# Output projections by seven half-sized block products, with the tick rebuilt for pairs of batches

## The chip, the cores and the metric

The kernel runs on one core of one Trainium2 chip. The time is device microseconds of one execution; medians of several executions are given, all in the fast state (runs within 1.5% of the fastest one of the same kernel). The kernel keeps all arithmetic in f32. Five engines matter: TensorE (PE; PEld is its weight load), VectorE (DVE), ScalarE (ACT), GpSimd (POOL) and the queue that starts transfers (SP).

## The reference, cut to what matters

128 graphs of 128 nodes with 512 features. Layer 0 is a transformer layer whose scores are multiplied by the adjacency matrix; layer 1 is a graph attention layer. Both are residual, with layer norm and a Relu ahead.

```python
# layer 0
h = relu(layernorm(x)); q, k, v = h @ Wq.T + bq, h @ Wk.T + bk, h @ Wv.T + bv   # 512 x 512 each
attn = softmax(q k^T * scale * (adj + adj)) per head (8 heads of 64)
x = x + (attn v) @ Wo.T + bo
# layer 1
h = relu(layernorm(x)); Wh = h @ W                                              # 512 x 512
e = leaky_relu(Wh a1 + (Wh a2)^T); e = where(adj > 0.5, e, -9e15)
x = x + elu(softmax(e, axis=1) @ Wh)
```

Both kernels reassociate layer 1: they first gather (attention times h) and then project with W. So each batch has five 512 x 512 projections: q, k, v, the output projection with Wo, and the last one with W.

## The kernel before

q, k and v are already done in the cheaper way: for a group of four batches, each of the three products is split into 2 x 2 blocks and formed from seven block products instead of eight (Winograd's form of Strassen's scheme). Sums of blocks are made on VectorE beforehand, and the results are put together from three banks of PSUM (the tiles `acc_a`, `acc_b` and `acc_c`, into which the products are accumulated). The 21 products ("units" q0 to v6) are strewn over the ticks of the group before, so that TensorE always has something independent to do. The output projections are plain:

```python
    def rows_matmul(lhsT, w):
        pm = ps1.tile([P, E], F32, name="pm", tag="ps1")
        for c in range(C):                       # 4 products of 128 x 512, f32
            nc.tensor.matmul(pm, lhsT[:, c, :], w[:, c, :], start=(c == 0), stop=(c == C - 1))
        return pm
    ...
        def done():                              # what follows a unit of q, k, v
            if n == 0:
                first(0, 0)                      # ScalarE: copy with bias out of bank "a"
            elif n == 1:
                add(0, 0, "b")                   # VectorE: add bank "b"
            ...
            elif n == 4:
                first(1, 1)                      # ScalarE, and then
                add(1, 1, "c")                   # VectorE, which waits for it
```

The schedule is written by hand, one tick per batch; in the trace VectorE runs its instructions in the order of the source (L380, L381 and L259, shown below, start at 1009.90, 1010.17 and 1010.43 us). The beginning of a tick (t is in attention, t-2 in layer 1):

```python
            if 0 <= t - 2 < B:
                scores1(t - 2)
                softmax1(t - 2)
            if t < B:
                scores(t)
                mask(t)
            done = unit(0)
            ...
            if 0 <= t - 2 < B:
                scale1(t - 2)        # scaling of the layer 1 attention w, needed by gather1
            done()                   # the end of unit 0, after it
            if t < B:
                exps(t)
            ...
            unit(1)()
            ...
            unit(2)()
            if 0 <= t - 2 < B:
                gather1(t - 2)       # TensorE: h2 times w
```

## Time and profile before

| | before |
|---|---|
| median | 2659.05 us (2658.74 to 2661.01, 3 runs) |
| TensorE busy, whole span / 100 to 2500 us | 98% / 100% |
| VectorE, ScalarE busy | 69%, 43% |
| period of four batches in the steady part | 81.14 us |
| clock of TensorE | 0.997 |

In this trace the granted clock of TensorE is 0.50 in a few stretches only: 3.41 us from 64.8 us on, 3.41 from 2607.8, 6.81 from 2641.9 and the last 0.25; from 68.3 to 2607.7 us it is 1.00. Such a fall to 0.50 is what the texts below mean by the clock gate, and by tripping it.

The prediction below shows the lines that carry this. This is VectorE around the scaling of w in a steady tick of the kernel before (columns: start, duration, engine, line, operation, output<-inputs, shape):

```profile
1009.90 0.15 DVE L380 RECIPROCAL rs<-sums 128x1 f32<-128x1 f32 x1
1010.17 0.34 DVE L381 TENSOR_SCALAR w<-w,rs,mv 128x128 f32<-128x128 f32 x1
1010.43 0.68 DVE L259 TENSOR_TENSOR kT<-acc_c,kT 128x512 f32<-128x512 f32 x1
```

The scaling (L381) stands ahead of the unit's add (L259), as in the source, and is done at 1010.5 us. The gather that needs it starts at 1015.95 us: over 5 us of slack. The order protected from little there: the units that begin a tick are q0, k0, k3 and k6, and of these only k6 ends with an add, which waits for no copy of its own unit.

### The profile page before, as it was taken

The numbers are of one execution on the slowest core, as the hardware profiler recorded it, in microseconds if no ns is written. First come the engines' busy times: TensorE is split into PE (matmuls) and PEld (weight loads), VectorE is DVE, ScalarE is ACT, GpSimd is POOL, SyncE is SP. The second block draws the span as 40 slices with busy tenths as digits, with TensorE's granted clock in tenths as the row PEclk, the third lists the DMA queues.
The fourth block names the chain that finished last, engine by engine and source line by source line (L and its number), as shares of the span: only waits on it lengthen the run. The fifth ranks groups of instructions, "written<-read, shape, count | busy, mean of one in ns | idle before, by whom it ended". The sixth has DMA issues, their size and how long they took to land.

```text
span 2655.8 us, 38303 instructions
## 1 busy us (share of the span) xinstructions
PE 2615.8 (98%) x13744; PEld 1882.8 (71%) x13744; DVE 1830.3 (69%) x3509; ACT 1151.3 (43%) x3595; POOL 334.7 (13%) x647
## 2 busy tenths in 40 slices
PE   7999999999999999999999999999999999999996
PEld 6677777777777777777777777777777777777763
DVE  5776767766676767677666767676776667676655
ACT  2444444444444444444444444444444444444443
POOL 1111111111111111111111111111111111111001
PEclk9999999999999999999999999999999999999999
DMA  4433322222321232222222223322222232122010
GB/s 153 68 74 70 64 64 64 65 64 66 77 56 57 74 70 64 64 65 63 64 67 77 58 54 75 69 64 64 66 62 64 67 77 58 55 75 57 31 40 20
DMA packets 209133, 173.29 MB, mean 65 GB/s; under 512 B 48432, under 2 KB 158000, under 8 KB 208560
## 3 DMA queue, kind: packets, MB, share of 16 engines
q1 hardware_dynamic: 207360, 170.84, 26.2%
q8 instruction: 109, 1.79, 0.4%
q14 instruction: 80, 0.66, 0.1%
q10 hardware_dynamic: 1584, 0.01, 0.0%
HBM read 137.11 MB, written 33.68 MB: 64 GB/s over the span
## 4 chain that ended last, share of the span: by engine, by line
PE 97%; DVE 2%; ACT 1%; DMA 1%; issue 0%; SPq 0%; ACTq 0%; DVEq 0%
PE pm L157 33%; PE acc_a L238 25%; PE acc_c L238 13%; PE acc_b L238 6%; PE sc L290 5%; PE pc L331 5%; PE pa L320 4%; PE pg L389 4%; PE pb L363 1%; ACT at L307 1%; DMA hT<-in_xT 0%; DVE at L314 0%; DVE nmx L300 0%; DVE at L296 0%; PE pt L177 0%; DMA x<-in_x 0%
## 5 line engine op out<-in xcount | busy, mean ns | idle before, releaser
L157 PE MATMUL pm<-w,gT 128*128 128x512 f32 x1024 | 464.0, 596 | 1.5 <-ACT gT L391 1.5
L157 PE MATMUL pm<-wo,cxT 128*128 128x512 f32 x1024 | 460.9, 593 | 0.5 <-ACT cxT L336 0.5
L307 ACT ACTIVATE at<-at,nmx 128x128 f32<-128x128 f32 x1024 | 395.6, 388 | 130.5 <-DVE nmx L300 130.5
L150 POOL TENSOR_SCALAR mv<-mv 128x1 f32<-128x1 f32 x256 | 117.1, 458 | 2149.8 <-DVE mv L147 2149.6
L157 PEld LDWEIGHTS pm<-w,gT 128*128 128x128 f32 x1024 | 195.4, 191 | 194.1 <-issue 185.9
L157 PEld LDWEIGHTS pm<-wo,cxT 128*128 128x128 f32 x1024 | 194.1, 190 | 191.1 <-issue 183.7
L399 DVE SCALAR_TENSOR_TENSOR x<-pm,x 128x512 f32<-128x512 f32 x128 | 88.5, 692 | 341.5 <-ACT ez L398 341.5
L398 ACT ACTIVATE ez<-pm 128x512 f32<-128x512 f32 x128 | 76.5, 598 | 399.2 <-PE pm L157 399.2
L238 PE MATMUL acc_a<-hT,wq 128*128 128x256 f32 x1024 | 246.7, 384 | 0.0
L238 PE MATMUL acc_a<-hT,wk 128*128 128x256 f32 x1024 | 245.3, 382 | 0.0
L238 PE MATMUL acc_a<-wv,hT 128*128 128x256 f32 x1024 | 244.2, 381 | 0.7 <-ACT v L250 0.7
L238 PEld LDWEIGHTS acc_a<-hT,wq 128*128 128x128 f32 x1024 | 190.7, 191 | 40.5 <-issue 14.8
L238 PEld LDWEIGHTS acc_a<-wv,hT 128*128 128x128 f32 x1024 | 189.4, 190 | 38.6 <-issue 14.8
L238 PEld LDWEIGHTS acc_a<-hT,wk 128*128 128x128 f32 x1024 | 187.2, 190 | 38.6 <-issue 14.8
L322 ACT COPY aT<-pa 128x1024 f32<-128x1024 f32 x128 | 129.6, 1012 | 147.4 <-PE pa L320 144.7
L307 ACT ACTIVATION_READ_ACCUMULATOR at<-at,nmx 128x1 f32 x1024 | 191.8, 187 | 0.0
L255 ACT ACTIVATE qT<-acc_a,bq 128x256 f32<-128x256 f32 x256 | 107.2, 470 | 194.6 <-PE acc_a L238 194.6
L145 DVE BATCH_NORM_STATS2 st<-x 128x6 f32<-128x512 f32 x256 | 176.4, 689 | 9.1 <-DMA x<-in_x 4.5
L151 POOL TENSOR_TENSOR mv<-mv,mhalf 128x1 f32<-128x1 f32 x256 | 177.3, 693 | 21.3
L331 PEld LDWEIGHTS pc<-aT,v 128*64 128x64 f32 x2048 | 109.2, 136 | 83.4 <-issue 83.4
L255 ACT ACTIVATE kT<-acc_a,bk 128x256 f32<-128x256 f32 x256 | 107.4, 471 | 134.0 <-PE acc_a L238 134.0
L314 DVE TENSOR_TENSOR at<-at,rs 128x1024 f32<-128x1024 f32 x128 | 156.8, 1225 | 4.4
(92 smaller groups left out, 3926.3 us busy)
## 6 DMA issues: line engine op xcount, KB each, us to landing
x<-in_x SPq DMA_DIRECT2D x256, 256.0 KB, 3.5
out<-x SPq DMA_DIRECT2D x128, 256.0 KB, 2.1
hT<-in_xT SPq DMA_DIRECT2D x120, 256.0 KB, 10.6
mr<-rows SPq DMA_DIRECT2D x120, 128.0 KB, 3.4
adj<-in_adj SPq DMA_DIRECT2D x128, 64.0 KB, 2.1
adjT<-in_adjT SPq DMA_DIRECT2D x128, 64.0 KB, 2.0
rows<-mv SPq DMA_DIRECT2D x120, 1.0 KB, 8.5
wq<-in_wqT SPq DMA_DIRECT2D x1, 1024.0 KB, 7.2
```

The costliest lines, as they stand in the source:

```text
L145: nc.vector.bn_stats(st, src)
L150: nc.gpsimd.tensor_scalar_add(rstd, rstd, EPS)
L151: nc.gpsimd.tensor_tensor(rstd, rstd, mhalf, OP.pow)
L157: nc.tensor.matmul(pm, lhsT[:, c, :], w[:, c, :], start=(c == 0), stop=(c == C - 1))
L238: nc.tensor.matmul(acc[:, m, :], lhsT, rhs, start=fresh and m == 0 and c == 0, stop=c == 1, skip_group_check=True)
L255: nc.scalar.activation(dst(t, f)[:, m, :], a[:, m, :], AF.Identity, bias=bias[:, j : j + 1])
L290: nc.tensor.matmul(sc[:, s * C + i, :], qT[r, i, cols], kT[r, i, cols], start=True, stop=True)
L307: nc.scalar.activation(at[:, j, :], at[:, j, :], AF.Exp, bias=nmx[:, j : j + 1], accum_out=sums[:, j : j + 1])
L314: nc.vector.tensor_tensor(at, at, rs[:, :, None].to_broadcast([P, H, S]), OP.mult)
L320: nc.tensor.transpose(pa[:, j, :], at[:, j, :], ident)
L322: nc.scalar.copy(aT, pa)
L331: nc.tensor.matmul(pc[s * D : (s + 1) * D, i, :], vs[b // G][:, b % G, head * D : (head + 1) * D], ats[b][:, s * C + i, :], start=True, st ...
```

## The change

Its intent: the two output projections, too, by seven block products. A block product needs two row blocks, so two batches go through a tick together. Now a pair's output projection is seven products of 128 x 256 over two K-blocks, instead of two times four of 128 x 512. In exchange VectorE makes the sums of blocks (`context_sums`, `gather_sums`) and adds the products up. Cut to its core:

```diff
-    def rows_matmul(lhsT, w):
-        ...
+    def product_rows(left, w, which, n):
+        la, wb, bank = PRODUCTS[n]
+        slot = 1 if bank == "b" else 0
+        own = "c" if bank == "c" else "a"
+        if n == 0 or n == 3:
+            accs[which, own] = ps1.tile([P, 2, E // 2], F32, name="row_" + own, tag="ps1")
+        acc = accs[which, own][:, slot, :]
+        for c in range(2):
+            nc.tensor.matmul(
+                acc, left[:, la, c, :], w[:, wb, c, :], start=n in (0, 3) and c == 0, stop=c == 1, skip_group_check=True
+            )
+        return acc
 ...
+    def context_sums(half):
+        token_sums(cxT, cxT[:, 4:7], (half,))
+    def output0(p, n):                                  # the adds of the first output projection
+        ...
+            if n == 0 or n == 1:
+                add(0, 0, acc)
 ...
-        nc.vector.tensor_scalar(h2, xs[b], mv[:, 0:1], 0.0, op0=OP.subtract, op1=OP.max)
+            nc.scalar.activation(h2[:, i, :], xs[p][:, i, :], AF.Relu, bias=nmr[:, i : i + 1], scale=mv[:, 1, i : i + 1])
 ...
+SEQ = "v0 v1 v2 v3 v4 q0 v5 q1 v6 q2 q3 q4 k0 q5 k1 q6 k2 k3 k4 k5 k6".split()
+            units = (SEQ[10:] if odd else SEQ[:10]) ...  # ten units in an even pair-tick, eleven in an odd one
+            if attn:
+                scores(a)                               # the mask and the maximum belong to it now
+            unit()()
+            if e is not None:
+                scores1(e)
+            if attn:
+                exps(a, range(4))
+            if o is not None:
+                first, second = output0(o, 0), output0(o, 1)
+                first()
+                second()
+            if e is not None:
+                softmax1(e)
+            if attn:
+                exps(a, range(4, H))
+            ...
+            unit()()
+            if e is not None:
+                scale1(e)
+            if o is not None:
+                output0(o, 2)()
+            done = unit()
+            if attn:
+                normalise(a)
+            done()
+            if f is not None:
+                finish_a(f)                             # final passes, one tick later than before
+            if e is not None:
+                gather1(e, 0)
+                gather1(e, 1)
+            done = unit()
+            if f is not None:
+                finish_b(f)
+            done()
 ...  (second half of the tick: batch b, products 3 to 6 of both projections, statistics, dots)
```

## The prediction

> **What bounds the kernel now.** I read the page first (busy shares, slices, chain), then the busy time of the steady stretch, the groups by form, and last the timeline of TensorE and of all engines.

> ```profile
> PE 2615.8 (98%) x13744; PEld 1882.8 (71%) x13744; DVE 1830.3 (69%) x3509; ACT 1151.3 (43%) x3595; POOL 334.7 (13%) x647
> ...
> PE 97%; DVE 2%; ACT 1%; DMA 1%; issue 0%; SPq 0%; ACTq 0%; DVEq 0%
> ```
> ```profile
> 100.00:2500.00 2400.00, 2400.00 (x12660) 1730.99 (x12659) 1683.48 (x3224) 1060.12 (x3323) 304.99 (x586) 1.00 0.27 65
> ```
> From 100 to 2500 us TensorE is busy in all 2400.00 us, at clock 1.00: it never waits, so the steady time is the sum of its passes. VectorE is busy in 70% of that stretch and ScalarE in 44%.
> ```profile
> 1007.24 1.99 PE L238 MATMUL acc_c<-hT,wk 128*128 128x256 f32 x8
> 1009.07 3.60 PE L157 MATMUL pm<-wo,cxT 128*128 128x512 f32 x8
> 1012.50 1.89 PE L238 MATMUL acc_a<-wv,hT 128*128 128x256 f32 x8
> 1014.23 1.89 PE L238 MATMUL acc_c<-wv,hT 128*128 128x256 f32 x8
> 1015.95 1.05 PE L389 MATMUL pg<-w,h 128*128 128x128 f32 x8
> 1016.84 1.89 PE L238 MATMUL acc_a<-wv,hT 128*128 128x256 f32 x8
> ```
> Read start to start: eight passes of 512 columns take 3.43 us (429 ns each), eight of 256 take 1.73 (216 ns each). A product in f32 is two passes.
> ```profile
> L307 ACT ACTIVATE at<-at,nmx 128x128 f32<-128x128 f32 x1024 | 395.6, 388 | 130.5 <-DVE nmx L300 130.5
> L314 DVE TENSOR_TENSOR at<-at,rs 128x1024 f32<-128x1024 f32 x128 | 156.8, 1225 | 4.4
> L255 ACT ACTIVATE qT<-acc_a,bq 128x256 f32<-128x256 f32 x256 | 107.2, 470 | 194.6 <-PE acc_a L238 194.6
> L366 DVE TENSOR_TENSOR w<-w,neg 128x128 f32<-128x128 f32 x128 | 36.6, 286 | 30.8 <-ACT w L365 30.8
> L259 DVE TENSOR_TENSOR v<-acc_c,v 128x512 f32<-128x512 f32 x64 | 44.0, 688 | 26.9 <-ACT v L250 23.8 <-PE acc_c L238 3.1
> ```
> These price the new small operations: on VectorE 128 columns cost 286 ns, 512 cost 688, 1024 cost 1225. So 256 columns, which do not occur before, should cost about 0.42 us (0.39 start to start).

> [...] the ratio 1:2 holds and halving a side loses nothing. [...] (1225-286)/896 = 1.05 ns per column. [...] VectorE's order in every tick is that of the source. This carries my main argument. [...] Seen here near the end: after 3.02 us of idling the next eight passes took 5.28 instead of 3.43 us, though after two equal gaps nothing happened.

> **The change, part by part.** I count in groups of four batches (two pairs), because 21 products of q, k, v belong to a group.

> *TensorE.* A batch has scores 1.09 + 0.19 of turnaround, context 1.03, the row transpose 0.25, gather 0.89, attention transpose 0.87: 4.32 us. The two output projections by the plain way are 2 x 3.43 = 6.86. A group: 4 x (4.32 + 6.86) + 21 x 1.73 = 81.05. Measured from the start of scores at 135.26 to that at 2569.39, 30 groups: 81.14. The method fits.
> After: each output projection of a pair is seven products of two K-blocks, two passes each, 28 passes of 256 columns = 6.06 us in place of 6.86. A group: 4 x 4.32 - 0.25 + 4 x 6.06 + 36.33 = 77.6. Gain 3.5 us a group, some 110 us of the run.

> *VectorE, per pair.* Added: sums of context blocks and of gathered blocks, 8 x 0.42; seven adds of output products in place of two of 684 ns, +1.57; three adds for the second projection, +1.26; the small product behind the statistics, +0.15. Gone: hidden1 moves to ScalarE (-0.96), the mask and its add become one operation (-0.6), and pairing saves on the residual, norm, shift, softmax and finishing operations (-1.3). Together +3.5 us on 28.6: 32 of some 39 us. The new small product after GpSimd's power also makes VectorE wait about 1 us a pair. ScalarE gains two Relu of 512 and four copies of 256, about +2.7 on 18. Neither becomes the bound by its sum.

> *DMA.* Bytes stay; fewer, larger transfers at a 27% share. Hidden.

> *Ends.* Before, outside those 30 groups: 2655.8 - 30 x 81.14 = 221.6. After: the weights' sums now stand ahead of the first hidden_T in VectorE's queue and wait for the load (+5); in the first two pairs some 10 us more of the output work is missing and moves to the end, and less idling is left there (-15); the drain is three pair-ticks of serial steps instead of two batch-ticks (+10). About 221. So the time is 221 + 30 x (77.6 + s), s being TensorE's new waiting in a group: 2549 with none.

> **What s is.** I followed the queues through a pair-tick in source order, with durations from the rows above. Zero is the start of the first batch's scores.

> End of an even tick: from the end E of the second attention transpose, ScalarE copies (1.0 + 0.1), makes the first half of h2 (0.7); VectorE does dots 1.36, add 0.39, dots 1.36, context_sums 0.78: E + 5.7. TensorE has two products of 0.87 and the context left: E + 2.8. So VectorE enters an odd tick 2.9 us behind TensorE. An odd tick has one more product (k6), which lets VectorE in at 1.9 in even ticks.

> Then the gather needs scale1. In an odd tick VectorE starts the mask at 2.9; mask and maximum 2.5, the new score operation 0.4; ScalarE: two Prelu 0.7, four exponentials at 0.387 = 1.55, two of the second softmax 0.8, four more 1.55, and then the two bias copies of product q4, 0.9. VectorE's add of q4 stands ahead of scale1 in its queue and must wait for those copies: 0.66, then reciprocal and scaling 0.66. TensorE starts the gather 0.26 later: at 2.9 + 10.0 = 12.9. In its own order it gets there after scores 1.1, q3 1.9, row transposes 0.35, two products 1.73, q4 1.73, one product 0.87, k0 1.73: at 9.4. It waits 3.5 us, once in each odd tick.
> In an even tick the second unit is v1, whose add waits for no late copy: scale1 is ready at about 1.9 + 7.0 = 8.9 against 9.4. No wait.
> At other places (attention transposes, sums ahead of the third output product, banks) I find slack of 0.5 to 8 us. So s = 3.5, and the gain of 3.5 a group is eaten almost whole: 221 + 30 x 81.1 = 2654.

> **The rivals.** (A) No new wait: TensorE stays gap-free, 2549. For it: all engines have room by their sums, and the order looks tuned by hand. Against it: even if VectorE began the mask as early as scores allow (1.2 instead of 2.9), the chain would end at 11.2, a wait of 1.8: 2603. (B) The waits are longer than I think: a gap of 3.5 us is in reach of the clock gate; if half the gaps cost another 1.85, +28 us: 2680. (C) VectorE becomes the bound in odd ticks (its list there: 36 us with the hidden sums and the wait for GpSimd, of 39.7): another 1.5 us a group of missed transposes or late bank releases, 2700. (D) The chain is real, but the next waits move, so that half is won back: 2600.

> **Range and chances.** The bare sum gives 2654. The clock gate pulls up, and the possibility that I misplace one wait in ScalarE's queue (an order this worked out has presumably been seen running well) pulls down harder. I say 2645, with 2590 to 2695. Faster by over 2% is below 2606: it needs s under 1.9, so 0.25. Slower by over 2% is above 2712: s above 5.4, 0.10. Within: 0.65.

> **What would show it.** Passes of 256 columns at 216 ns in both output projections: the gain exists. TensorE's steady stretch no longer fully busy, with the idle time ahead of the gather (pg), put down to VectorE's scaling of w, about 3.5 us, in every second pair-tick and not in the others: my step is right. If the gather never waits, or waits in both kinds of tick, the chain is wrong. VectorE should show 78 to 82% busy, with a wait for GpSimd of 1 us a pair; the mean clock below 0.99 would mean the gate took part. A time near 2550 overturns the argument; one above 2700 says that VectorE's queue binds at more places than this one.

## The result

| | before | after |
|---|---|---|
| median (4 runs each) | 2658.89 us | 2704.13 us |
| span of the profiled run | 2655.8 us | 2701.3 us |
| TensorE busy | 2615.8 us, 98% | 2554.2 us, 95% |
| VectorE, ScalarE busy | 69%, 43% | 76%, 48% |
| period of four batches | 81.14 us | 82.66 and 81.17 us in turn |

The ratio is 1.0173 (1.0155 to 1.0191): slower by 1.7%. Here and below a ratio is the mean time of one kernel's fast runs over that of the other's fast runs of the same rounds, so not quite the ratio of the medians. TensorE is busy for 62 us less, though some of its passes now run at half speed (below). All of that, and 45 us more, went into waiting. The slowdown is clear of noise, but smaller than the 2% at which the record calls a kernel slower.

The page of the kernel after, busy shares and chain:

```profile
PE 2554.2 (95%) x15288; PEld 2184.8 (81%) x15288; DVE 2052.4 (76%) x3781; ACT 1306.0 (48%) x3915; POOL 119.1 (4%) x263
...
PE 77%; DVE 10%; ACT 9%; issue 3%; DMA 1%; POOL 0%; SPq 0%; POOLq 0%; DVEq 0%; ACTq 0%
```

The chain that ended last (followed back from the last instruction, each step to what released it) was 97% TensorE before. Now it runs through VectorE and ScalarE for 19% of the span. This alone doesn't size the loss: in e10 below, where TensorE's steady part shows no wait, it is still 16%. Of the groups (busy time and mean ns of one, then the idle time ahead and its releaser), the new products and the gather:

```profile
L297 PE MATMUL row_a<-wo,cxT 128*128 128x256 f32 x1280 | 323.3, 383 | 10.9 <-DVE x L370 10.7
L297 PE MATMUL row_a<-w,gT 128*128 128x256 f32 x1280 | 319.2, 380 | 1.8 <-ACT z L474 0.9
L447 PE MATMUL pg<-w,h 128*128 128x128 f32 x1024 | 156.0, 316 | 97.7 <-DVE w L439 94.7
```

The block products are as fast as those of q, k and v and almost never wait. The gather (L447) waits 94.7 us in 32 places for VectorE's scaling of w (L439), and its mean pass has gone from 276 ns before to 316. Two gathers of odd pair-ticks, one after the other, with the unit that follows each:

```profile
1005.30 2.02 PE L447 MATMUL pg<-w,h 128*128 128x128 f32 x16 [2.98 <-DVE w L439]
1007.15 1.89 PE L245 MATMUL acc_a<-hA,wq 128*128 128x256 f32 x8
...
1086.47 3.50 PE L447 MATMUL pg<-w,h 128*128 128x128 f32 x16 [2.99 <-DVE w L439]
1089.82 1.89 PE L245 MATMUL acc_a<-hA,wq 128*128 128x256 f32 x8
```

Both waited the same 2.98 to 2.99 us. The first took 1.85 us to the next unit, the second 3.35: it ran at half speed. The busy times in the stretch of each of these two gathers (columns: stretch, length, busy us of PE, PEld, DVE, ACT, POOL, then clock, share of the transfer engines, GB/s):

```profile
1005.30:1008.70 3.40, 3.40 (x24) 3.22 (x25) 3.33 (x5) 1.17 (x2) 0.00 (x0) 1.00 0.00 0
1086.40:1089.80 3.40, 3.33 (x16) 3.36 (x17) 3.33 (x5) 0.58 (x1) 0.00 (x0) 0.53 0.00 0
```

The clock there is 1.00 and 0.53. In the steady part every second gap is followed by such a stretch; that is why the periods alternate between 81.17 and 82.66 us.

```profile
1000.84:1004.25 3.41, 1.47 (x7) 0.95 (x5) 0.32 (x1) 3.41 (x17) 0.00 (x0) 1.00 0.00 0
1082.76:1086.17 3.41, 0.72 (x4) 0.29 (x2) 1.03 (x3) 3.03 (x13) 0.00 (x0) 1.00 0.00 0
```

So it is in all 30 gaps from 186 to 2561 us: the 15 that tripped the clock have 2.50 to 2.70 us in one step, the 15 others 1.95 at most. This is read from one trace; no run shifted the gaps to test it. Nor is it a sharp limit: in the drain a step with two waits, 1.83 us of idling in all (2656.31 to 2659.72), tripped the clock too.

In even pair-ticks there is no wait at all:

```profile
1045.03 1.95 PE L447 MATMUL pg<-w,h 128*128 128x128 f32 x16
```

The wait itself, step by step, in one odd pair-tick that starts with the scores at 1074.04 us (engines mixed, in order of time):

```profile
1076.98 1.22 DVE L314 SCALAR_TENSOR_TENSOR at<-sc,adj 128x1024 f32<-128x1024 f32 x1
1078.23 1.22 DVE L318 TENSOR_REDUCE nmx<-at 128x8 f32<-128x1024 f32 x1
1079.37 0.41 DVE L421 SCALAR_TENSOR_TENSOR w<-adjT,pb 128x256 f32<-128x256 f32 x1
1079.81 0.69 ACT L423 ACTIVATE w<-w,ws 128x128 f32<-128x128 f32 x2 [2.40 <-DVE w L421]
...
1082.34 0.39 ACT L432 ACTIVATE w<-w,nmx 128x128 f32<-128x128 f32 x1
...
1084.26 0.81 ACT L262 ACTIVATE qT<-acc_a,bq 128x256 f32<-128x256 f32 x2
1085.11 0.69 DVE L266 TENSOR_TENSOR qT<-acc_c,qT 128x512 f32<-128x512 f32 x1 [4.15 <-ACT qT L262]
1085.71 0.15 DVE L438 RECIPROCAL rs<-sums 128x2 f32<-128x2 f32 x1
1085.90 0.42 DVE L439 TENSOR_TENSOR w<-w,rs 128x256 f32<-128x256 f32 x1
```

The second exponential of layer 1's softmax (L432) ends at 1082.7 us. From then on the scaling could run. But VectorE stands in front of q4's add (L266) for 4.15 us until ScalarE, behind four more exponentials, has made q4's copies (L262). Only then come the reciprocal and the scaling.

### The profile page after: what moved, and what is told of

It reads as the page before. It is cut to its first block, busy times and chain, and to the rows that moved or that the text cites. A ratio compares the mean times of both kernels' runs of the same rounds, so it can differ in the third digit from the quotient of the medians.

```text
span 2701.3 us, 40548 instructions
## 1 busy us (share of the span) xinstructions
PE 2554.2 (95%) x15288; PEld 2184.8 (81%) x15288; DVE 2052.4 (76%) x3781; ACT 1306.0 (48%) x3915; POOL 119.1 (4%) x263
## 4 chain that ended last, share of the span: by engine, by line
PE 77%; DVE 10%; ACT 9%; issue 3%; DMA 1%; POOL 0%; SPq 0%; POOLq 0%; DVEq 0%; ACTq 0%
PE acc_a L245 20%; PE row_a L297 16%; PE acc_c L245 10%; PE row_c L297 8%; PE acc_b L245 6%; PE pg L447 6%; PE pa L336 4%; ACT at L324 4%; PE sc L312 4%; DVE junk L409 4%; PE pc L356 4%; DVE at L314 2%; ACT aT L338 1%; ACT w L432 1%; ACT w L423 1%
## 5 line engine op out<-in xcount | busy, mean ns | idle before, releaser
L297 PE MATMUL row_a<-wo,cxT 128*128 128x256 f32 x1280 | 323.3, 383 | 10.9 <-DVE x L370 10.7
L297 PE MATMUL row_a<-w,gT 128*128 128x256 f32 x1280 | 319.2, 380 | 1.8 <-ACT z L474 0.9
L297 PEld LDWEIGHTS row_a<-wo,cxT 128*128 128x128 f32 x1280 | 236.0, 191 | 48.6 <-DVE x L370 20.6
L297 PEld LDWEIGHTS row_a<-w,gT 128*128 128x128 f32 x1280 | 236.2, 191 | 31.1 <-ACT z L474 1.7
L447 PE MATMUL pg<-w,h 128*128 128x128 f32 x1024 | 156.0, 316 | 97.7 <-DVE w L439 94.7
L262 ACT ACTIVATE kT<-acc_a,bk 128x256 f32<-128x256 f32 x256 | 106.9, 469 | 290.9 <-PE acc_a L245 290.9
L447 PEld LDWEIGHTS pg<-w,h 128*128 128x128 f32 x1024 | 149.8, 230 | 112.3 <-ACT kT L262 100.8
L262 ACT ACTIVATE qT<-acc_a,bq 128x256 f32<-128x256 f32 x256 | 106.6, 466 | 125.3 <-PE acc_a L245 125.3
L330 DVE TENSOR_TENSOR at<-at,rs 128x1024 f32<-128x1024 f32 x128 | 156.8, 1225 | 4.4
L318 DVE TENSOR_REDUCE nmx<-at 128x8 f32<-128x1024 f32 x128 | 156.2, 1220 | 4.4
L370 DVE TENSOR_TENSOR x<-row_a,x 128x256 f32<-128x256 f32 x320 | 135.2, 422 | 31.0 <-PE row_a L297 24.5
L314 DVE SCALAR_TENSOR_TENSOR at<-sc,adj 128x1024 f32<-128x1024 f32 x128 | 154.4, 1206 | 4.5 <-PE sc L312 4.5
L312 PE MATMUL sc<-kT,qT 64*128 64x128 f32 x2048 | 149.7, 286 | 0.0
L266 DVE TENSOR_TENSOR qT<-acc_c,qT 128x512 f32<-128x512 f32 x64 | 44.0, 688 | 134.0 <-ACT qT L262 130.8
```

The costliest lines, as they stand in the source:

```text
L262: nc.scalar.activation(dst(t, f)[:, m, :], a[:, m, :], AF.Identity, bias=bias[:, j : j + 1])
L297: nc.tensor.matmul(acc, left[:, la, c, :], w[:, wb, c, :], start=n in (0, 3) and c == 0, stop=c == 1, skip_group_check=True)
L312: nc.tensor.matmul(sc[:, s * C + j, :], qT[r, j, cols], kT[r, j, cols], start=True, stop=True)
L314: nc.vector.scalar_tensor_tensor(at, sc, QSCALE, adjs[p][:, i : i + 1, :].to_broadcast([P, H, S]), op0=OP.mult, op1=OP.mult)
L318: nc.vector.tensor_reduce(nmx, at, AX.X, OP.max, negate=True)
L330: nc.vector.tensor_tensor(at, at, rs[:, :, None].to_broadcast([P, H, S]), OP.mult)
```

## The experiments

Two theories stood against each other. **Queue**: one wrong place in VectorE's order costs a gap, and the gap trips the clock gate (a stretch of 3.41 us at clock 0.50 in the trace above). **Sum**: with 3.5 us more a pair VectorE is near its bound, so that a wait taken away at one place comes back at another. All ten kernels gave the right result. The median of the kernel before was 2658.9 to 2663.5 us in the four sets of rounds, so a difference of medians from different sets can be off by some 5 us; ratios and, for small differences, the periods in the traces don't have this fault.

### e1: the scaling ahead of the unit's add

```diff
-            unit()()
-
+            done = unit()
             if e is not None:
                 scale1(e)
+            done()
```

> Only the order within the second unit is changed: the scaling of w (scale1) is issued ahead of the copies and the add that end that unit. Queue theory (the gather of an odd pair-tick waits 3.1 us because scale1 stands behind the add of q4, which waits for ScalarE's copies, and every second such gap also trips the clock gate for 1.5 us): the scaling ends 2.8 us earlier, a wait of about 0.4 us is left, no gate; 2704 - 31 x 2.7 - 22 = about 2600 us. Rival, VectorE is the bound by its sum and the wait only moves: over 2670 us, with new idle time of TensorE elsewhere in the tick.

Measured: 2609.29 us, ratio to before 0.9796 (0.9779 to 0.9812). One line moved makes the kernel 95 us faster than the change as given. The odd pair-tick now:

```profile
1128.29 2.02 PE L447 MATMUL pg<-w,h 128*128 128x128 f32 x16
1130.14 1.89 PE L245 MATMUL acc_a<-hA,wq 128*128 128x256 f32 x8
1132.22 1.09 PE L336 MATMUL pa<-ident,at 128*128 128x128 f32 x8 [0.18 <-DVE at L330]
```

The gather no longer waits for anything the profile names; 0.18 us is left ahead of the attention transpose. The period is 78.72 us in every group: the alternation has gone with the gap. The queue theory's 2600 is missed by 9 us (e8 takes another 0.4 us off each group), the sum theory's "over 2670" by 60.

### e2, e3: the gather moved behind the fourth unit, alone and with e1

```diff
-            if e is not None:
-                gather1(e, 0)
-                gather1(e, 1)
             done = unit()
             if f is not None:
                 finish_b(f)
             done()
+            if e is not None:
+                gather1(e, 0)
+                gather1(e, 1)
```

> Only the gather is moved behind the fourth unit on TensorE (1.73 us of independent passes); VectorE's and ScalarE's order up to scale1 stays. Queue theory: the wait falls from 3.1 to 1.4 us in odd ticks, the gate no longer trips; 2704 - 31 x 1.73 - 22 = about 2628 us. Rival, VectorE is the bound: VectorE's order ahead of the gather is the same and it would be no faster, over 2685 us.

> Both edits together. Queue theory: no wait ahead of the gather in any tick, groups of four batches at 77.6 us; 2704 - 31 x 3.1 - 22 = about 2585 us. Rival, VectorE is the bound or the next wait stands close behind: over 2650 us, with the idle time ahead of another operation.

Measured: 2641.88 us (ratio 0.9917) and 2641.77 us (ratio 0.9916). e2 was 14 us slower than expected. e3 was 57 us slower than the queue theory had it, and worse than e1 alone: by its number alone it speaks more for the sum theory ("over 2650"). The profile of e3 shows what it is, in every odd pair-tick:

```profile
1143.49 1.99 PE L245 MATMUL acc_a<-hA,wq 128*128 128x256 f32 x8 [1.64 <-ACT qT L262]
1145.32 1.95 PE L447 MATMUL pg<-w,h 128*128 128x128 f32 x16
```

This is q5, which now comes before the gather. It accumulates on in the bank that q4's copies (L262) are still reading, and waits 1.64 us for them. e2 shows the same wait, 42.7 us in 26 places between 300 and 2400 us, as e3 does. With the gather ahead of it, this second wait had stood hidden. So it is a new wait on the same late copies, not a full VectorE, but that had to be tested: e10.

### e10: e3, with q4's copies ahead of the second four exponentials

```diff
+            done = unit(early=True)        # product 4 makes its copies at once, its add stays in done()
             if attn:
                 exps(a, range(4, H))
             if p == 1:
                 spread_u()
-            done = unit()
```

> On the kernel of e3: the two bias copies of q4 are issued on ScalarE ahead of the second four exponentials instead of behind them; nothing else moves. In e3 product q5 waits 1.64 us in each odd tick for those copies to leave its bank. If that is what e2 and e3 missed: the wait goes and no other takes its place, groups at 78.3 us, 2642 - 31 x 1.6 = about 2592 us. If the wait for the bank has another cause or a third wait stands behind it: over 2625.

Measured: 2595.36 us, ratio 0.9742 (0.9729 to 0.9755), period 78.32 us, against 79.85 in e3. The second wait was the copies' place in ScalarE's queue, and no third stood behind it.

### e4: the gap filled, not shortened

Six products of constant weights, issued into the gather's own bank, which the gather overwrites:

```diff
+        if fill:                            # odd ticks only
+            for _ in range(6):
+                nc.tensor.matmul(
+                    pg[:, 0:2, :].rearrange("p c s -> p (c s)"), wo_sb[:, 0, 0, 0:P], wo_sb[:, 1, 0, :], start=True, stop=True
+                )
```

> Nothing is moved; in odd ticks six products of constant weights (12 passes of 256 columns, 2.6 us) are issued ahead of the gather into its own bank, which the gather then overwrites. They fill the gap of 3.1 us without shortening it. Gate theory (the idle time trips the clock, which costs 1.5 us in every second group): the slow stretches in the steady part vanish, all groups at 81.2 us, 2704 - 15 x 1.5 = about 2682 us. Rival, the slow stretches have another cause (they come every 163.8 us anyway): 2704 us or more, with the half-speed gathers still there.

Measured: 2681.69 us. The edited kernel's line numbers are shifted (L448 is the filling, L452 the gather):

```profile
996.21 2.75 PE L448 MATMUL pg<-wo 128*128 128x256 f32 x12
999.36 2.02 PE L452 MATMUL pg<-w,h 128*128 128x128 f32 x16 [0.40 <-DVE w L439]
1001.22 1.89 PE L245 MATMUL acc_a<-hA,wq 128*128 128x256 f32 x8
```

The steady groups from the second on all take 81.17 us: the gap costs as much as before, but no half-speed stretch follows it. So idling causes the stretches, and in the steady part they cost 2704.13 - 2681.69 = 22 us (and 15 x 1.49 by the periods). It is a strange cure, useless work that makes a kernel faster, and a good test.

### e5, e6: the same VectorE operation added at two places

On e1's kernel, the maximum over the scores is taken twice, for the second batch of the pair (e5) or for the first (e6). It adds 1.22 us a pair-tick, 78 us of VectorE's work, either way.

```diff
-        nc.vector.tensor_reduce(nmx, at, AX.X, OP.max, negate=True)
+        for _ in range(2 if i == 1 else 1):          # e6: i == 0
+            nc.vector.tensor_reduce(nmx, at, AX.X, OP.max, negate=True)
```

> On the kernel of e1: the maximum over the scores of the second batch of every pair is computed twice (one more VectorE operation of 1.22 us a pair-tick, 78 us over the run, same result), where attention transposes have some 3 us of slack. Queue theory: at most 10 us more than e1's 2609. Rival, VectorE is the bound by its sum once the gather's wait is gone: 2609 + 64 x 1.22 = some 2685 us.

> The same operation of 1.22 us, as often, but on the first batch of the pair, ahead of the chain to the gather. Queue theory: even ticks have 0.5 us of slack and odd ones none, so 0.7 + 1.3 us a group: 2609 + 31 x 2.0 = about 2670 us, the wait ahead of the gather again. If only VectorE's sum counted, the time would equal e5's.

Measured: 2613.80 us and 2667.02 us: 5 and 58 us more than e1. The period is 78.72 us in e5, as in e1, and 80.54 in e6. VectorE is busy in 81% and 80% of the span. So its sum isn't the bound; where an operation stands decides. A part of my expectation for e6 was wrong: the wait is not ahead of the gather but earlier, at the third product of the first output projection (L371 is VectorE's add of the two products before it, out of the same bank):

```profile
505.32 1.13 PE L297 MATMUL row_a<-wo,cxT 128*128 128x256 f32 x4 [1.08 <-DVE x L371]
512.24 1.10 PE L337 MATMUL pa<-ident,at 128*128 128x128 f32 x8 [0.18 <-DVE at L331]
```

I had traced that bank in the change and found it just free in time; with 1.22 us more ahead of the adds it isn't. That the time still came within 3 us of my 2670 was luck.

### e7, e8, e9: the first pair-tick, and the best version

The ends of the run had also come out longer than predicted. In the first pair-tick of e1 VectorE stands 7.2 us (5.7 in the change as given) in front of a load (`hidden`) while the second batch's softmax waits behind it. e7 is e1 with that call moved behind the residual shift, in the first pair-tick only.

```diff
-            if h is not None:
+            if h is not None and p > 0:
                 hidden(h)
 ...
                 shift(p)
             done()
+            if p == 0:
+                hidden(h)
```

> On the kernel of e1: in the first pair-tick alone, the first use of a loaded xT (it waits 7.2 us for its transfer, in front of the second batch's softmax in VectorE's queue) is issued after the residual shift. If this wait makes the first ticks longer than I had them: the 5.6 us idle ahead of the second attention transpose goes and the half-speed stretch after it with it, 8 to 10 us: about 2600. If the first ticks are long for another reason: within 2 us of e1's 2609.

Measured: 2607.62 us, 2 us under e1: no gain worth naming. The wait had moved to the next operation in VectorE's queue that needs a transfer, the statistics of a later pair:

```profile
78.12 0.69 DVE L159 BATCH_NORM_STATS2 st<-x 128x6 f32<-128x512 f32 x1 [8.68 <-DMA x<-in_x]
```

e8 adds two edits to e7: the first batch's `normalise` also goes ahead of the second unit's add (which in e1 still waits 1.63 us for ScalarE), and the sums of w1's blocks move to the second pair-tick.

```diff
             if attn:
                 normalise(a)
+            done2()                        # the end of the second unit, now behind scale1 and normalise
             done()
 ...
-                weight_sums(w1_sb)         # at the end of the first pair-tick
 ...
+            if p == 1:
+                weight_sums(w1_sb)         # in the middle of the second
```

> The best version I can see: e1, with the normalisation of the first batch also issued ahead of the add of the second unit, e7's edit, and the sums of w1's blocks one tick later. Queue theory: groups at 78.2 us instead of 78.7 (-16), first ticks shorter (-10): about 2585 us, faster than the kernel before by 2.8%. If VectorE's queue binds elsewhere: 2600 or more.

Measured: 2594.77 us, ratio 0.9747 (0.9733 to 0.9762). The period falls to 78.32 us (78.2 expected); the first ticks gain 2 us of the 10 I had hoped for. e9 also moves that tick's statistics (`stats0`, `spread0`) behind the shift:

> On the kernel of e8: in the first pair-tick the row statistics of a later pair, which in e7 took over the wait for a transfer (8.7 us), are also issued after the residual shift. If VectorE's two waits for loads made that tick long: the 4.5 us idle ahead of the second attention transpose and the half-speed stretch after it go, 6 to 9 us, about 2587 us. If not: within 2 us of e8's 2595.

Measured: 2589.72 us, ratio 0.9720 (0.9706 to 0.9733), 5 us better than e8. The attention transpose of the first pair's second batch, e8 and then e9:

```profile
87.47 1.94 PE L336 MATMUL pa<-ident,at 128*128 128x128 f32 x8 [4.48 <-DVE at L330]
```
```profile
83.66 1.06 PE L336 MATMUL pa<-ident,at 128*128 128x128 f32 x8 [0.17 <-DVE at L330]
```

The 4.48 us of idle time are down to 0.17 and the transpose takes 1.06 us in place of 1.94; the first four batches take 71.7 us instead of 76.2. This is the fastest version: 2.8% under the kernel before.

## Why the prediction was right or wrong

The measured 2704 lies above the range of 2590 to 2695. The mechanism of the wait was right and was found ahead of the run. Two terms of the sum were mis-sized, and then I moved my own sum to the wrong side.

**The wait (right).** The place (ahead of the gather), the cause (the scaling behind q4's add, which waits for q4's copies), the kind of tick (odd only) and even VectorE's entry into the odd tick (predicted 2.9 us after the scores start, measured 1076.98 - 1074.04 = 2.94) are as predicted. The profile puts the wait at 2.99 us, and 3.14 us pass from the end of k0 (1.73 us after its start) to the gather's start, against 3.5. e1 shows the cause: only the order of that add and the scaling changed.

**The floor of 77.6 us a group (a little low).** In e8, e9 and e10, where hardly any wait is left, it is 78.3. This and the smaller wait cancel, by luck: 81.17 us measured for a group without the gate, 81.1 predicted.

**The clock gate (mis-sized: this is the first failing term).** I had it as rival B, "if half the gaps cost another 1.85, +28 us", and left it out of the sum. Half the gaps did (15 of 30): 1.5 us each, 22 us by e4. The 1.85 came from a mixed reading: 5.28 us is a duration, 3.43 a time from start to start; from start to start the slow passes took 2613.01 - 2607.80 = 5.21, so 1.78 more.

**The ends (mis-sized: the second failing term).** "About 221" us outside the 30 groups. Measured: the scores that begin the groups counted start at 134.16 and 2593.06 us, so 2701.3 - 2458.9 = 242.4. The start of the first scores was right (56.91 us, predicted as 51.94 + 5). But my "-15" for the first group was too hopeful: it took 77.25 us, when I had expected 83.3 - 15 = 68. Part of that is VectorE waiting for transfers in its first tick (e9 took 4.5 us off this group against e8), part the half-speed stretch around it (10.2 us from 86.1 us on, at clock 0.50). The drain took 108.2 us against 86.4 + 10 = 96; the clock is 0.91 and 0.88 in the last two stretches that I measured, 2560 to 2640 and 2640 to 2702 us. I ran nothing that splits the drain's 12 us further.

**The sum.** 2654 + 22 (gate) + 21 (ends) + 3 (rest) = 2700, for a span of 2701.3.

**The range.** The step "the possibility that I misplace one wait ... pulls down harder" was the worst. It set a general belief (a kernel this worked out will run well) against a chain that I had followed instruction by instruction, and closed the range at 2695 when my own sum with rival B stood at 2680. The 0.65 for a time within 2% of the kernel before came true, but on the slower side; my 2645 was on the faster one.

**The signs.** The clock below 0.99, the sign for the gate, came (0.983). A time above 2700 was to say that VectorE's queue binds at more places than one. It came too, but that reading was wrong: in the steady part (300 to 2400 us) the profile names no wait of TensorE but the gather's, and the excess is the gate and the ends.

**The rivals.** A (no wait, 2549) fell with the gap; even with the waits gone the period is 78.3 and the ends are longer. C (VectorE bound in odd ticks) fell with e1 and e5; that its 2700 is the nearest number is an accident. D (half won back) did not happen in the change. That VectorE would be 78 to 82% busy was near (76%), and its added work was right: (2052.4 - 1830.3) / 64 = 3.47 us a pair, 3.5 predicted. The wait for GpSimd was there: 72.7 us in 64 pair-ticks, 1.1 each.

**Where the expected gain went.** The new products do their part: from 81.14 to 78.3 us a group, 85 us of the run. The change as given lost this to a gap of 3 us in every second pair-tick (81.17), to the gate that the gap trips (22 us), and to 21 us more outside the groups than the kernel before has, of which e9 wins back some.

## What to carry to other kernels

Here VectorE's order mattered before its sum did. So, when an engine gets full, list what stands ahead of each operation that the bound engine waits for, and whether any of it waits for a third engine. The kernel before had the scaling on the safe side of the add; the rebuilt tick had lost that detail and put a unit with late copies there, and one moved line was worth 95 us. And an idle gap of 3 us on TensorE cost 1.5 us beyond its length in every second case, so put the gate into the sum and not among the rivals.

## What the runs showed of the clock and of shared banks

- Gaps of 2.99 us by the profile (3.14 from the end of one unit to the next start) tripped the clock gate in exactly every second of 30 cases: 2.50 to 2.70 us of idling inside one step of 3.413 us were enough here, and once, in the drain, 1.83.
- The kernel's period and the steps of the clock ran together here: two groups with one half-speed stretch take 82.66 + 81.17 = 163.83 us, and the trace's clock records put the stretches 163.84 us apart and 3.41 us long, 48 stretch lengths.
- The gap can be filled where it can't be closed: 12 passes of products whose result is overwritten took 22 us off the run (e4).
- A 128 x 256 product in f32 was two passes of 216 ns here.
- Accumulating several products in one place and reading it in between had a price: the next product waited until the reader's queue got there, 1.64 us in each odd pair-tick of e3 (where the copies read the very elements that the product adds to) and 1.08 in e6.
